# Moving the writes of turned tiles from SyncE's DMA queue to ScalarE's, and exchanging two PSUM banks

## Chip, core and metric

The kernel runs on one core of one Trainium2 chip. The metric is device time in microseconds (us) of one execution. Engines are named as in the profile: PE is TensorE (PEld its weight loads), DVE is VectorE, ACT is ScalarE, POOL is GpSimd and SP is SyncE. A "q" behind an engine's name (SPq) means its sequencer, which issues DMAs.

## What is computed

The input `x` is 128 graphs of 128 nodes with 512 features, in float32; `adj` is one 128x128 adjacency matrix for all of them. Two layers follow each other, each of the form "normalise, ReLU, graph operation, add to the input":

```python
# layer 0: graph convolution
h = relu(layernorm(x))
x = x + norm_adj @ (h @ W) + b          # norm_adj = D^-1/2 adj D^-1/2
# layer 1: attention with 8 heads of 64, masked by the adjacency
h = relu(layernorm(x))
q, k, v = h @ Wq + bq, h @ Wk + bk, h @ Wv + bv
a = softmax(q @ k.T / 8 + (1 - adj) * -1e9)
x = x + (a @ v) @ Wo + bo
```

## The kernel before

**Tiling.** A graph is one *element* of the batch. Four elements make a *group* (`GB = 4`), and there are 32 groups. The five 512x512 projections of a group are done by a Winograd form of Strassen's scheme (seven block products, most of them with seven products inside again), so that PE does fewer multiplications, and DVE and POOL do the additions.

**Order.** The schedule is written by hand. For each slot `t` the program runs five blocks, W, Q, K, V and Y: W is the graph convolution's product for group t+1, Q, K and V are the attention projections of group t, and Y is the output projection of group t-1. Each block has seven steps, 0 to 6, and each step has places for other work before it (`"Q3"`), between its two parts (`"Q3b"`) and after them (`"Q3c"`). The table `plan` says what else is done at a place: `at(t, "Q3c", f, ...)` appends a call. So five groups are in the air at a time: while PE projects group t, the softmax of group t-1 ends, its attention matrices are turned, and at V0 they are multiplied with v (`attend`, L943), right after K's last step and right before the scores of group t (`scores`, L868).

**Turning.** The attention product needs the attention matrices with keys on the partitions. Instead of transposes on PE, most groups are turned in two halves. `flip_att` (L917, L918) has DVE transpose all 32x32 blocks of the element's 128x1024 tile `att`, and then writes the tile to a DRAM buffer (`turned<-att`, one DMA of 512 KB). `turn_att` waits for that write and reads it back with the blocks exchanged (`att<-turned`, four DMAs of 128 KB by `from_dram`, L789, whose runs in DRAM are 32 floats long). The normalised input h of the attention layer is turned in the same way for two elements at a time: `flip_h` (L776, L778) and `turn_h`, with the DRAM buffers `h_dram` (`turned_h<-att`, `turned_h<-op_o`, `op_h<-turned_h`). Group 0 turns elements 2 and 3, and the last group all, on PE.

**DMA.** All DMAs are issued by SP, in program order: the turned writes and reads, five parts of 512 KB of each of the four weights for every group (`w<-wd_q` and so on, L1133), two loads of `x` (L177) and two stores of the result (L962). An instruction that waits on SP holds up all DMAs behind it. The built program also gives its DMAs eight completion semaphores in turn, and each DMA waits until the one eight places before it in the program has landed, whichever engine issued it.

**Banks.** There are eight PSUM banks: a0, a1, d0, d1, b, c with fixed names, and two small ones that take turns (`small_bank`). `attend` runs over the elements in the order 2, 0, 1, 3. Elements 2 and 3 write to a small bank, element 0 to bank b and element 1 to the a-bank that K's step 5 used last. Before PE may write bank b or that a-bank, DVE must have added K's results in them to `k`: these reads are L481 (parts of a bank) and L496 (a whole bank), at the end of block K. ACT copies the attention products out of PSUM (`fill`, L407). The scores of element 1 then go to bank b and the same a-bank, and those of element 3 to the two small banks.

**ACT in block Q.** In this order: two copies of q (L811), the statistics of an `x` tile (L340 and L341, twice), copies of q, two ReLUs with the normalisation (`gcn_norm`, L372, `h<-op_o`), two more pairs of statistics, copies of q and of `op_a` (L407), the third ReLU. `gcn_mix` on PE (tile `pa`, L142) reads each of those h.

Of the kernel before, what the change touches and what calls it, by code (L numbers as in the profile page):

```python
# [97 lines left out]
def kernel(  # L98
# [16 lines left out]
    nc = tc.nc  # L115
# [6 lines left out]
    NG = B // GB  # L122
# [21 lines left out]
    def small_bank(name):  # L144
        return ps_t.tile([P, 512], F32, tag="bank", name=name)
# [4 lines left out]
    bank = {k: ps_c.tile([P, 512], F32, tag=f"bank_{k}", name=f"bank_{k}") for k in ("a0", "a1", "d0", "d1", "b", "c")}  # L150
    turn = [0]
# [7 lines left out]
    att_dram = [dp.tile([P, H * P], F32, tag=f"turned_{b}", name=f"turned_{b}") for b in range(GB)]  # L159
    h_dram = [dp.tile([P, H * P], F32, tag=f"turned_h_{y}", name=f"turned_h_{y}") for y in range(2)]  # L160
# [609 lines left out]
    def flip_h(g, b):  # L770

        half, j = divmod(b, 2)
        h2 = hs.pop((g, b)).rearrange("n (c i f) -> n c i f", c=NC, i=4)
        t = op_att.t[:, SLOTS - 12 : SLOTS - 4, :] if half else att_of(g - 2, 2 if g > 2 else 1)
        t = t.rearrange("p s n -> p (s n)")
        nc.vector.transpose(t.rearrange("n (i c j f) -> n j c i f", i=4, c=NC, j=2)[:, j], h2)  # L776
        if j:
            nc.sync.dma_start(h_dram[half], t)  # L778

    def turn_h(g, half):  # L780
        op_h[g] = op_norm
        first = LEFT_AT[S1 if half else A11]
        from_dram(op_norm.t[:, first : first + 8, :], h_dram[half])
# [46 lines left out]

    maxima, sums = {}, {}

    def att_of(g, b):


        return att_buf[(b if g == 0 else b + 4 - 2 * g) % (GB + 1)]

    def by_blocks(g, b):  # L840

        return 0 < g < NG - 1 and not turned_in_place(g, b)

    def weights_of(g, b):

        return att_of(g, b - 1 if 0 < g < NG - 1 else b)

    def turned(g, b):

        if turned_in_place(g, b):  # L850
            return weights_of(g, b)
        return att_of(g, b - 2 if g else b - 1)

    def turned_in_place(g, b):

        return g == NG - 1 or g == 0 and b >= 2
# [55 lines left out]
    def flip_att(g, b):  # L912

        t = turned(g, b).rearrange("q h k -> q (h k)")
        order = "q h (i k) -> q h i k" if by_blocks(g, b) else "q h (k i) -> q h i k"
        dst = t.rearrange("q (i h k) -> q h i k", i=4, h=H)
        nc.vector.transpose(dst, weights_of(g, b).rearrange(order, i=4))  # L917
        nc.sync.dma_start(att_dram[b], t)  # L918

    def turn_att(g, b):  # L920
        from_dram(turned(g, b), att_dram[b])
# [10 lines left out]
    def attend(g, b):  # L932
        if g not in op_o:
            op_o[g] = op_norm if g == NG - 1 else op_att
        aT = turned(g, b)
        if b == 2 or b == 3:
            po = small_bank(f"po_{g}_{b}")
        else:
            po = bank["b" if b == 0 else f"a{1 - turn[0]}"]
        for c in range(NC):  # L940
            for p in range(2):
                h = 2 * c + p
                nc.tensor.matmul(  # L943
                    po[p * HD : (p + 1) * HD, c * P : (c + 1) * P],
                    vs[g][:, b, h * HD : (h + 1) * HD],
                    aT[:, p * NC + c, :],
                    start=True,
                    stop=True,
                )
        op_o[g].fill(nc.scalar.copy, b, po)  # L950
# [18 lines left out]
    def at(slot, place, f, *args):  # L969
        plan.setdefault((slot, place), []).append((f, *args))  # L970

    for t in range(-1, NG + 1):


        last = t == NG - 1
        if 0 <= t - 1 < NG - 1:
            g = t - 1

            for first, final, place, f, *args in (
                ("W4", "-Y6c", "W1c" if t == 2 else "-Y6c", flip_att, 0),  # L980
                ("W6", "Q2", "W4" if t == 2 else "W3", turn_att, 0),
                ("Q4c", "Q1c", "Q0b", flip_att, 1),
                ("Q6", "Q3", "Q2b", turn_att, 1),
                ("W6", "-Y3", "-Y3", exponentials, 2, 0, H // 2),
                ("Q3c", "-Y4", "-Y4", exponentials, 2, H // 2, H),
                ("Q6b", "-Y5b", "W0c" if t == 2 else "-Y5b", softmax_end, 2),
                ("K0c", "-Y5", "-Y5", exponentials, 3, 0, H // 2),
                ("K1c", "-Y6", "-Y6", exponentials, 3, H // 2, H),
                ("K3c", "W0", "W2", softmax_end, 3),
                ("K1", "Q2c", "Q2c", flip_att, 2),  # L990
                ("K3", "Q4", "K0", turn_att, 2),
                ("K3", "Q3c", "Q4b", flip_att, 3),
                ("K5", "Q5", "K0b", turn_att, 3),
            ):
                place = first if t == 1 else final if last else place
                if f in (flip_att, turn_att) and turned_in_place(g, args[0]):
                    continue
                at(t - place.startswith("-"), place.strip("-"), f, g, *args)
            if t == 1:
                at(1, "K4", transpose_att, g, 2)  # L1000
                at(1, "K6", transpose_att, g, 3)
            for b in (2, 0, 1, 3):
                at(t, "V0", attend, g, b)
        if t == 0:

            at(0, "Q0b", ln2, 1, 0)
            at(0, "Q1b", ln2, 1, 1)
            at(0, "K6", norm_h, 1, 0)
            at(0, "K6", norm_h, 1, 1)
            at(0, "V4", transpose_h, 1, 0)  # L1010
            at(0, "V4", norm_h, 1, 2)
            at(0, "V5", transpose_h, 1, 1)
            at(0, "V5", norm_h, 1, 3)
            at(1, "W0", transpose_h, 1, 2)
            at(1, "W1", transpose_h, 1, 3)
            at(1, "W1b", attention_operands, 1)
            at(2, "Q5", attention_residual, 1, 0)
            at(2, "K1", attention_residual, 1, 1)
        elif 1 <= t + 1 < NG and t >= 0:
            g = t + 1  # L1020
            at(t, "Q3b" if g < NG - 1 else "Q0b", ln2, g, 0)
            at(t, "K0b" if g < NG - 1 else "Q3b", ln2, g, 1)
            if g == NG - 1:

                places = ("Q3", "Q4", "Q5", "Q5", "Q6", "Q6", "K1", "K2", "K2")
                steps = ((norm_h, 0), (norm_h, 1), (transpose_h, 0), (norm_h, 2), (transpose_h, 1), (norm_h, 3))
                steps += ((transpose_h, 2), (transpose_h, 3))
            else:
                places = ("K1c", "K2c", "K4c", "K5b", "K3", "K4b", "K6b", "K6b", "Y6b")
                if t == 1:  # L1030
                    places = ("K2c", "K3c", "K6", "K6b", "K4b", "K5b", "V0b", "V0b", "Y6b")
                steps = ((norm_h, 0), (norm_h, 1), (norm_h, 2), (norm_h, 3))
                steps += tuple((flip_h, b) for b in range(GB))
                for half in range(2):
                    at(t, ("V3", "Y0")[half], turn_h, g, half)
            for place, (f, b) in zip(places, steps):
                at(t, place, f, g, b)
            at(t, places[8], attention_operands, g)
            at(t + 1, "Q3", attention_residual, g, 0)
            at(t + 1, "Q4", attention_residual, g, 1)  # L1040
# [3 lines left out]
        if 3 <= t + 2 < NG:  # L1044
            place = (t - 1, "Y6b") if t > 1 else (t, "W0")
            at(*place, load_x, t + 2, (0,), t > 1)
            at(*place, load_x, t + 2, (1,), t > 1)
        if 2 <= t + 2 < NG:
            g = t + 2
# [13 lines left out]
        if 0 <= t < NG:  # L1063
            g = t
# [30 lines left out]
        if last:  # L1095
            g = t
            at(t, "Y0", row_max, g, 2)

            at(t + 1, "W0", combine_w, "o last", nc.gpsimd)
            at(t, "Y1", exponentials, g, 2, 0, H)  # L1100
            at(t, "Y1b", row_max, g, 3)
            at(t, "Y2b", softmax_end, g, 2)
            at(t, "Y3", exponentials, g, 3, 0, H)
            at(t, "Y4b", softmax_end, g, 3)
            at(t, "Y6", transpose_att, g, 2)
            at(t + 1, "W0", transpose_att, g, 3)
            for b in range(GB):
                at(t + 1, "W0", attend, g, b)
            at(t + 1, "W0", output_operands, g)

            at(t + 1, "Y4", store_half, g, 0, slice(0, 256))
            at(t + 1, "Y5", store_half, g, 0, slice(256, 512))
            at(t + 1, "Y6", store_half, g, 1, slice(256, 512))
# [204 lines left out]
```

## Time and profile before

| | |
|---|---|
| median of 3 runs | 2262.12 us (2257.41 to 2262.69) |
| the profiled execution | 2243.55 us, of which the core's span is 2241.8 us; granted PE clock 0.999 |
| PE busy | 2200.8 us (98% of the span) |
| DVE, POOL, ACT busy | 1884.1 us (84%), 1868.6 us (83%), 1285.5 us (57%) |
| SP's DMA queue | 594.20 MB; its packets took 91.2% of 16 DMA engines' span |
| one group, from attention product to attention product | 67.9 to 68.2 us in 17 of the 27 of the steady stretch, 69.2 to 70.6 us in the other 10 |

The row of the profiled execution is what the profile's views describe; its time is below the three timed runs by 18.57 us at the median. "Idle before" in the views is time in which the engine did nothing before an instruction, and behind "<-" stands what ended most of it. Lines are of the kernel before.

### The profile page before, as it was taken

To read this page: it belongs to the slowest core of one execution; us is meant where nothing else is said; L and a number is where in the kernel's file an instruction comes from. 1 tells how busy PE (TensorE), PEld (TensorE's weight loads), DVE (VectorE), ACT (ScalarE), POOL (GpSimd) and SP (SyncE) were. 2 spreads that over 40 slices of the span, in tenths; PEclk is the share of its full clock that TensorE was granted. 3 is DMA by queue.
4 is the path that set the end of the run, shared out by engine and by line. 5 is a ranking of instruction groups with operands and counts; after the bars stand their busy time and mean duration, and the time that the engine had idled before them with its cause. 6 is when DMAs were issued, how large, how long until landed. Compare 5 with 4: busy or idle time off the path is not lost.

```text
span 2241.8 us, 78690 instructions
## 1 busy us (share of the span) xinstructions
PE 2200.8 (98%) x31597; PEld 1877.0 (84%) x31597; DVE 1884.1 (84%) x4252; ACT 1285.5 (57%) x3813; POOL 1868.6 (83%) x1994
## 2 busy tenths in 40 slices
PE   9989999999999999999999999999999999999999
PEld 6777888888888888888888888888888888888887
DVE  7787888888888888888888878888888888888886
ACT  3566655656556556566565575655665655756444
POOL 6898888888888988889888888888898888898764
PEclk9999999999999999999999999999999999999999
DMA  5389999999999999999999999999999999999994
GB/s 162 142 259 274 276 292 272 252 279 273 297 283 284 262 263 293 257 298 262 286 268 294 272 249 293 266 301 272 284 272 291 268 295 283 271 282 284 259 251 173
DMA packets 908108, 599.23 MB, mean 267 GB/s; under 512 B 765664, under 2 KB 772960, under 8 KB 907104
## 3 DMA queue, kind: packets, MB, share of 16 engines
q1 hardware_dynamic: 907744, 594.20, 91.2%
q8 instruction: 250, 4.10, 0.8%
q14 instruction: 114, 0.93, 0.1%
HBM read 455.68 MB, written 138.41 MB: 265 GB/s over the span
## 4 chain that ended last, share of the span: by engine, by line
PE 81%; DVE 7%; DMA 6%; SPq 3%; issue 1%; POOL 1%; ACT 1%; DVEq 0%; POOLq 0%
PE bank_a L142 31%; PE bank_d L142 18%; PE bank_b L142 10%; PE bank_c L142 9%; PE pa L142 4%; SPq L789 3%; DVE k L481 3%; PE bank_d L868 3%; DMA turned<-att 3%; DMA att<-turned 2%; PE po L943 2%; DVE q L481 2%; PE pss L868 1%; PE bank_b L868 1%; PE bank_b L943 1%
## 5 line engine op out<-in xcount | busy, mean ns | idle before, releaser
L899 ACT ACTIVATE att<-att,nmx 128x128 f32<-128x128 f32 x1024 | 402.9, 506 | 2.2 <-DVE nmx L887 1.5
L910 POOL TENSOR_TENSOR att<-att,rsm 128x1024 f32<-128x1024 f32 x121 | 229.5, 1897 | 149.3 <-DVE rsm L904 124.5
L142 PE MATMUL bank_a<-op_h,w 128*64 128x256 f32 x2976 | 352.8, 379 | 0.0
L811 ACT ACTIVATE q<-bank_a,bqk 128x256 f32<-128x256 f32 x192 | 79.9, 466 | 438.7 <-PE bank_a L142 438.7
L481 DVE TENSOR_TENSOR xt<-xt,bank_d 128x512 f32<-128x512 f32 x610 | 270.6, 468 | 11.8 <-PE bank_d L142 0.8
L142 PEld LDWEIGHTS bank_a<-op_h,w 128*64 128x64 f32 x2976 | 207.5, 137 | 81.6 <-issue 0.2
L94 POOL TENSOR_TENSOR op_o<-op_o 128x256 f32<-128x256 f32 x297 | 213.9, 739 | 27.2 <-DVE v L481 10.2
L142 PE MATMUL bank_d<-op_h,w 128*64 128x128 f32 (+1 forms) x3424 | 221.7, 275 | 0.0
L899 ACT ACTIVATION_READ_ACCUMULATOR att<-att,nmx 128x1 f32 x1024 | 211.0, 206 | 0.0
L94 POOL TENSOR_TENSOR op_a<-op_a 128x256 f32<-128x256 f32 x279 | 197.9, 733 | 15.1 <-ACT v L825 5.4
L142 PEld LDWEIGHTS bank_d<-op_h,w 128*64 128x64 f32 x3424 | 195.1, 137 | 6.7 <-issue 0.2
L94 POOL TENSOR_TENSOR op_h<-op_h 128x256 f32<-128x256 f32 x270 | 191.0, 731 | 9.4
L372 ACT ACTIVATE h<-xt,nb,rs 128x512 f32<-128x512 f32 x142 | 173.3, 1226 | 16.9 <-POOL nb L357 15.2
L142 PE MATMUL bank_a<-w,op_o 128*64 128x256 f32 x1536 | 182.2, 379 | 0.0
L142 PE MATMUL bank_a<-w,op_h 128*64 128x256 f32 x1488 | 178.0, 381 | 0.0
L142 PE MATMUL bank_a<-w,op_a 128*64 128x256 f32 x1488 | 176.5, 379 | 0.0
L496 DVE TENSOR_TENSOR xt<-bank_a,xt 128x512 f32<-128x512 f32 x252 | 165.9, 679 | 2.8 <-PE bank_a L142 2.8
L825 ACT COPY v<-bank_a 128x512 f32<-128x512 f32 x96 | 56.2, 585 | 181.9 <-PE bank_a L142 143.4
L887 DVE TENSOR_REDUCE nmx<-att 128x8 f32<-128x1024 f32 x128 | 152.5, 1209 | 0.6 <-POOL att L883 0.6
L917 DVE STREAM_TRANSPOSE att<-att 128x1024 f32<-128x1024 f32 x122 | 152.5, 1250 | 0.3 <-ACT att L899 0.2
L875 DVE SCALAR_TENSOR_TENSOR att<-bank_d,msk 128x512 f32<-128x512 f32 x128 | 82.4, 685 | 82.8 <-PE bank_d L868 82.7
L377 POOL TENSOR_TENSOR xt<-xt,b_o 128x1024 f32<-128x1024 f32 x62 | 147.5, 2381 | 0.0
(198 smaller groups left out, 5851.1 us busy)
## 6 DMA issues: line engine op xcount, KB each, us to landing
w<-wd_v SPq DMA_DIRECT2D x155, 512.0 KB, 6.5
w<-wd_o SPq DMA_DIRECT2D x155, 512.0 KB, 9.9
w<-wd_q SPq DMA_DIRECT2D x150, 512.0 KB, 5.3
w<-wd_k SPq DMA_DIRECT2D x150, 512.0 KB, 7.6
turned<-att SPq DMA_DIRECT2D x122, 512.0 KB, 5.2
att<-turned SPq DMA_DIRECT2D x488, 128.0 KB, 4.0
out_dram<-xt SPq DMA_DIRECT2D x62, 512.0 KB, 5.0
op_h<-turned_h SPq DMA_DIRECT2D x232, 128.0 KB, 4.9
```

Source lines behind the costliest of these rows:

```text
L94: engine.tensor_tensor(twice(out), twice(x), twice(y), ALU.subtract if minus else ALU.add)
L142: nc.tensor.matmul(out[y : y + P // 2], lhsT[:, y : y + P // 2], rhs, **flags)
L372: nc.scalar.activation(dst, src, AF.Relu, bias=nb[:, j : j + 1], scale=rs[:, j : j + 1])
L377: engine.tensor_tensor(t, src, bias.unsqueeze(1).to_broadcast([P, t.shape[1], D]), ALU.add)
L481: nc.vector.tensor_tensor(dst, dst, src, f)
L496: nc.vector.tensor_tensor(t, src.rearrange("p (r f) -> p r f", r=2), t, ALU.add)
L868: nc.tensor.matmul(pss[p][:, c, :], qs[g][rows, c, cols], ks[g][rows, c, cols], start=True, stop=True)
L875: nc.vector.scalar_tensor_tensor(dst, pss[p], SCALE, mask, ALU.mult, ALU.add)
L887: nc.vector.tensor_reduce(nmx, att_of(g, b), AX.X, ALU.max, negate=True)
L899: nc.scalar.activation(dst, src, AF.Exp, bias=nmx[:, h : h + 1], scale=1.0, accum_out=sm[:, h : h + 1])
L910: engine.tensor_tensor(att, att, rsm.unsqueeze(2).to_broadcast([P, H, P]), ALU.mult)
L917: nc.vector.transpose(dst, weights_of(g, b).rearrange(order, i=4))
```

## The change

All turned writes from the second group on, and the writes of turned h from the fourth group's h on, are taken from SP and issued by ACT. The DVE transposes stay where they are. A new function `write_turned` issues a write at a place of its own: for the attention of elements 0 to 3 at Y6c of the slot before, and at Q1, Q3c and Q5 (for the first such group W3 instead of Y6c; for the last one Y6c, Q2c, Q3c, Q4c), for h at K5b and V0. Before, SP had them at the places of the transposes, elements 0 to 3 at Y6c, Q0b, Q2c and Q4b. In the built program 176 DMAs go from SP's stream to ACT's; PE, DVE and POOL have the same instructions in the same order. The order of the elements in `attend` stays 2, 0, 1, 3, but element 0 now writes to a small bank and element 3 to bank b (in all groups but the last).

```diff
@@ flip_h
-        if j:
+        if j and g == 2:
             nc.sync.dma_start(h_dram[half], t)
+        elif j:
+            turned_to_dram["h", half] = t
+
+    def write_turned(kind, n):
+
+        dram = h_dram if kind == "h" else att_dram
+        nc.scalar.dma_start(dram[n], turned_to_dram.pop((kind, n)))
@@ flip_att
-        nc.sync.dma_start(att_dram[b], t)
+        if g == 0:
+            nc.sync.dma_start(att_dram[b], t)
+        else:
+            turned_to_dram["att", b] = t
@@ attend
-        if b == 2 or b == 3:
+        if b in ((2, 3) if g == NG - 1 else (0, 2)):
             po = small_bank(f"po_{g}_{b}")
         else:
-            po = bank["b" if b == 0 else f"a{1 - turn[0]}"]
+            po = bank[f"a{1 - turn[0]}" if b == 1 else "b"]
@@ the plan
                 at(t - place.startswith("-"), place.strip("-"), f, g, *args)
+                if f == flip_att and t > 1:
+                    b = args[0]
+                    place = (("-Y6c", "Q2c", "Q3c", "Q4c") if last else ("W3" if t == 2 else "-Y6c", "Q1", "Q3c", "Q5"))[b]
+                    at(t - place.startswith("-"), place.strip("-"), write_turned, "att", b)
@@ the plan, h of group t + 1
+            if 1 < t and g < NG - 1:
+                at(t, "K5b", write_turned, "h", 0)
+                at(t, "V0", write_turned, "h", 1)
```

More of the change, by code (lines that the diff above doesn't have):

```diff
@@ L827, in values @@
         return Projection(lambda: op_h[g], "v", region, False, first, g > 0).steps()
-    maxima, sums = {}, {}
+    maxima, sums, turned_to_dram = {}, {}, {}
     def att_of(g, b):
```

## The prediction

> **What bounds the kernel now.** I read the page first, then PE's groups with their shapes, SP's waits, the windows from one attention product to the next, and last the timeline around two of these products. The page's lines on engines, queue and chain:
>
> ```profile
> PE 2200.8 (98%) x31597; PEld 1877.0 (84%) x31597; DVE 1884.1 (84%) x4252; ACT 1285.5 (57%) x3813; POOL 1868.6 (83%) x1994
> ...
> q1 hardware_dynamic: 907744, 594.20, 91.2%
> ...
> PE 81%; DVE 7%; DMA 6%; SPq 3%; issue 1%; POOL 1%; ACT 1%; DVEq 0%; POOLq 0%
> ...
> turned<-att SPq DMA_DIRECT2D x122, 512.0 KB, 5.2
> ```
>
> PE is the bound: of 2241.8 us it is idle in 41.0. DMA is the next one, with 91.2%. Where PE is idle, by its groups (busy, mean ns | idle before):
>
> ```profile
> L943 PE MATMUL po<-att,v 128*64 128x128 f32 x1024 | 68.8, 277 | 21.2 <-DMA att<-turned 16.9 <-issue 3.8 <-PE bank_a L943 0.4
> ...
> L943 PE MATMUL bank_b<-att,v 128*64 128x128 f32 x512 | 35.4, 280 | 4.4 <-DVE k L481 4.4
> ```
>
> So 25.6 us of the 41.0 lie before the attention products, 21.2 of them before elements 2 and 3, whose matrices come late from DRAM. Why late, by SP's own waits (total, times, longest):
>
> ```profile
> SPq L789 <- DMA turned<-att: 286.4, 90, 9.0
> ```
>
> SP stands 286.4 us waiting for turned writes to land before it can read them back. The windows between attention products show what it costs (PE, PEld, DVE, ACT, POOL busy; clock; DMA share; GB/s):
>
> ```profile
> 902.77:972.47 69.70, 67.86 (x993) 58.41 (x993) 58.88 (x135) 40.22 (x119) 58.83 (x64) 1.00 0.95 272
> ...
> 1041.94:1109.86 67.92, 67.65 (x997) 58.38 (x995) 58.62 (x135) 40.24 (x119) 58.54 (x63) 1.00 0.95 279
> ...
> sum 1852.37, PE 1830.44 PEld 1578.02 DVE 1579.18 ACT 1085.75 POOL 1582.32; mean PE 67.79 PEld 58.45 DVE 58.49 ACT 40.21 POOL 58.60
> ```
>
> There are 27 such windows in the steady stretch. 17 take 67.9 to 68.2 us, 10 take 69.2 to 70.6. The late ones have the same work; DMA is not full in them (0.95), it waits. SP's timeline in a late one:
>
> ```profile
> 935.03 0.34 SPq L918 DMA_DIRECT2D turned<-att  x1
> ...
> 945.64 2.97 SPq L789 DMA_DIRECT2D att<-turned  x4
> ...
> 961.35 2.17 SPq L918 DMA_DIRECT2D turned<-att  x2
> ...
> 965.92 6.85 SPq L789 DMA_DIRECT2D att<-turned  x8
> ```
>
> Element 0's write takes 10.6 us to land, behind the loads of x and weights that SP issued before. All that follows on SP is late by that: the transposes of elements 2 and 3 end at 952.11 and 955.16 on DVE, yet their writes go out at 961.35, because the read of element 1 stands before them on SP. Their reads begin at 965.92, and the last one lands after PE wants it.
>
> **The change, part by part.** *The 176 moved writes.* On SP they go away: per group six issues of 0.319 to 2.250 us (median 0.377), and with them SP's wait for the transpose. No SP instruction is on PE's path except through landings. On ACT, the write of element 0 finds ACT idle (14.34 us before the next copy of q). It no longer queues behind SP's backlog. How long a write takes to land in a queue of its own no row shows. The bounds are 2.7 us (shortest landing of a turned tile in the trace) and the median 5.2 us. I take 4.2, the median over turned writes and reads together, which is nearest to a write with little before it. Then element 0's read can begin at about 939 instead of 945.64. The write of element 2 goes out at its place on ACT, when the two `h<-op_o` are under way (951.75 to 953.27): 8 us before 961.35. Element 3's goes out behind two more pairs of statistics, at about 956: 6 us earlier. Their reads still stand in SP's order and take 6.85 to 7.60 us of issue. Lateness at PE is 3.4 us at most in one group, so 4 to 6 us earlier covers every group: the 10 late windows become like the others, if DMA has the time. Its share of 0.93 to 1.01 of 67.9 us leaves 5 us to nothing. I therefore expect a few groups to stay late and keep 2.7 us of the stalls.
>
> [...] No run here has shown two queues.
>
> *What ACT pays.* Per group 6 x 0.377 = 2.3 us of issue, on an engine busy 40.2 of 67.9 us. The writes at Y6c, K5b and V0 lie where it idles (14.34 us, and 3.26 us before the first attention copy). Those at Q1, Q3c and Q5 (1.1 us) lie in a stretch that is full:
>
> ```profile
> 957.71 0.82 ACT L372 ACTIVATE h<-op_o,nb,rs 128x512 f32<-128x512 f32 x1 [0.17 <-POOL nb L354]
> ```
>
> This third h ends at 958.53, and PE's next `pa` starts at 958.73: 0.20 us of slack. The price lies between 0 (the sequencer issues while the activation before it runs) and 1.1 - 0.2 = 0.9 us per group, 25 us over 28 groups. ACT's rows start before the one before has ended (953.70 against 953.18 + 0.62), so its sequencer runs ahead. I take 0.1 us per group, 3 us. Queued behind each write on ACT are copies of q that DVE adds to, statistics that POOL's `nb` waits for, and that h.
>
> *The new waits on ACT.* Each write waits for its transpose (which ends before ACT arrives, by the times above) and for the DMA eight places before. For element 2 that is the second of three `w<-wd_k`. In the clean group it is issued at 1017.80 and lands 6.9 us later, at 1024.7, while ACT arrives by 1024.48. After the change it no longer stands behind element 1's write (issued at 1017.42, when its transpose ended) and goes out right after 1014.91, so it lands near 1022: no wait. I cost it at nothing; the cover is these 2 us, and every microsecond without it goes to PE.
>
> *The exchange of banks.* In a clean group PE waits at bank b, but DVE reads the a-bank right after it:
>
> ```profile
> 1042.80 0.41 DVE L481 TENSOR_TENSOR k<-k,bank_b 128x256 f32<-128x256 f32 x1
> ...
> 1043.26 0.85 PEld L943 LDWEIGHTS bank_b<-att,v 128*64 128x64 f32 x16 [0.51 <-DVE k L481]
> 1043.26 1.09 PE L943 MATMUL bank_b<-att,v 128*64 128x128 f32 x16 [0.27 <-DVE k L481]
> 1043.32 0.68 DVE L496 TENSOR_TENSOR k<-bank_a,k 128x512 f32<-128x512 f32 x1
> ...
> 1044.18 1.04 PE L943 MATMUL bank_a<-att,v 128*64 128x128 f32 x16
> ```
>
> With element 0 in a small bank, element 1 would reach the a-bank at 1043.69, but DVE leaves it at 1044.00. It starts at 1044.05 instead of 1044.18. So the 4.4 us at bank b mostly turn into a wait at the a-bank; 0.13 us per group is gained. Element 3 in bank b is read by ACT 0.78 us after its last matmul begins to drain, and the scores need that bank 0.9 us after: no wait, but little room.
>
> *Sum,* against the profiled execution. The 27 windows would take 27 x (67.91 - 0.13) = 1830.1 instead of 1852.37: 22.3. The stall before the first of them is 3.4. Less 2.7 for groups that stay late and 3 for ACT: 20.0 us, 2223.6 from 2243.55. The timed runs are 18.57 us above that execution. If this is a constant, the median becomes 2242.1. If it is ten more late groups at about 1.8 us each, it goes too: 2223.6. No view decides between them, and I take the middle, 2233.
>
> **The rivals.** *ACT is held (slower).* If weights land later in the timed runs than in the clean group, element 2's write holds ACT. In the late group that `w<-wd_k`, issued at 950.79, lands 7.4 us later at 958.2, and ACT arrives at 953.27: 4.9 us. Beyond 0.2 us it all falls on `pa`. At 1.5 us per group: 28 x 1.3 = 36 us lost against 20 gained, 2278. It decides from 20 / 28 + 0.2 = 0.9 us per group. For it: the slack of 0.2 us. Against it: the weights come earlier too, as their hold-up was element 0's read.
>
> [...]
>
> *DMA is full anyway (no change).* The bytes are the same. If the engines have no time left, as the share of 0.97 to 1.01 in several clean groups may mean, reads get later as writes get earlier, and only the banks' 28 x 0.13 = 3.6 us remain: 2258.5. Against it: the late windows have 0.93 to 0.96, less than the clean ones.
>
> **How the numbers follow.** About 0.3% (6.8 us) is what a measurement can tell from no change. Forecast 0.74, full DMA 0.10, held ACT 0.16. The low end is all stalls gone and the excess with them, 2243.55 - 25.7 = 2217.9; the high end takes in the second rival and a held ACT at break-even, 2262. That leaves out the held ACT beyond it.
>
> **What would show it.** Right: `turned<-att` under ACTq landing in under 5.2 us; SP's 286.4 us much smaller; `po<-att,v` idle 21.2 down to 5 or less; all windows near 67.8; bank b's idle gone and some 0.2 us before `bank_a<-att,v`. Wrong: `pa` or q's banks waiting for ACT, or windows still at 69 to 70 us with the reads as late as now.

## The result, and the profile after

The changed kernel takes 2294.62 us at the median (2292.56 to 2297.75), the kernel before 2259.76 us (2255.82 to 2262.69) on the same chip: 1.0157 times as long, with a 95% interval of 1.0134 to 1.0179. It is slower by 34.86 us, where 2233 us, a gain, were predicted. The profiled execution took 2295.67 us (span 2293.9 us, granted PE clock 0.994), 52.1 us more than the profiled one of before. The timed medians differ by less because the kernel before's profiled execution (2243.55 us) is some 16 us below the median that it has here; which part of the 52.1 us the timed executions lack is not shown.

The page's lines on engines, queues (q1 is SyncE's, q10 ScalarE's), chain and writes of turned tiles:

```profile
PE 2219.5 (97%) x31597; PEld 1885.8 (82%) x31597; DVE 1885.7 (82%) x4252; ACT 1292.5 (56%) x3813; POOL 1868.0 (81%) x1994
...
q1 hardware_dynamic: 882400, 501.91, 77.7%
q10 hardware_dynamic: 25344, 92.29, 10.3%
...
PE 69%; DVE 13%; DMA 7%; ACT 4%; issue 2%; POOL 2%; SPq 2%; ACTq 0%; DVEq 0%; POOLq 0%
...
turned<-att ACTq DMA_DIRECT2D x120, 512.0 KB, 6.0
```

At the median the writes land in 6.0 us from a queue of their own, where they took 5.2 behind everything on SyncE. PE is busy for 18.7 us more with the same matmuls, and idle for 33 us more. PE's groups, with their shapes (busy, mean ns | idle before):

```profile
L142 PE MATMUL bank_d<-op_h,w 128*64 128x128 f32 x3360 | 220.8, 278 | 0.0
L142 PE MATMUL pa<-ant,h 128*64 128x128 f32 x2032 | 134.7, 282 | 48.2 <-ACT h L372 48.2
L953 PE MATMUL po<-att,v 128*64 128x128 f32 x1024 | 61.5, 273 | 0.0
L953 PE MATMUL bank_a<-att,v 128*64 128x128 f32 x512 | 34.9, 278 | 5.3 <-DVE k L496 5.2
L953 PE MATMUL bank_b<-att,v 128*64 128x128 f32 x512 | 33.7, 274 | 6.3 <-DMA att<-turned 4.7 <-issue 0.9 <-DMA turned_h<-att 0.7
```

The 21.2 us before `po` are gone, and bank_a waits 0.19 to 0.20 us in 26 of 28 groups, as predicted. But `pa` waits 48.2 us for the third h, where it waited 2.8. SP waits longer than the 286.4 us of before, not less:

```profile
SPq L796 <- DMA turned<-att: 407.8, 61, 11.0
```

Three of the windows between attention products (PE, PEld, DVE, ACT and POOL busy; clock; DMA share; GB/s), and the sum over the same 27 as before:

```profile
428.81:500.60 71.79, 69.53 (x997) 59.95 (x994) 58.70 (x135) 40.82 (x119) 58.53 (x63) 0.98 0.92 276
...
850.93:923.55 72.62, 69.53 (x996) 59.96 (x994) 58.70 (x135) 40.61 (x119) 60.16 (x64) 0.98 0.93 274
...
1066.10:1134.72 68.62, 67.86 (x997) 58.29 (x995) 58.69 (x135) 39.70 (x119) 58.59 (x63) 1.00 0.94 275
...
sum 1904.53, PE 1848.34 PEld 1586.51 DVE 1584.13 ACT 1093.53 POOL 1582.59; mean PE 68.46 PEld 58.76 DVE 58.67 ACT 40.50 POOL 58.61
```

The sum is 52.2 us above before (1904.53 - 1852.37), which is all of the difference between the two profiles. PE's busy time has 17.9 us of it (1848.34 - 1830.44). The rest is idle time: 45.4 more before `pa`, 5.3 before bank_a, 1.9 more before bank_b, 21.2 less before `po`, and small waits.

Why h is late is seen in ScalarE's timeline of the second of these windows (start, duration; in brackets the idle time before):

```profile
899.78 1.52 ACT L372 ACTIVATE h<-op_o,nb,rs 128x512 f32<-128x512 f32 x2 [0.23 <-POOL nb L354]
903.98 0.34 ACTq L785 DMA_DIRECT2D turned<-att  x1
904.42 0.63 ACT L340 ACTIVATE unused<-op_o 128x512 uint8<-128x512 f32 x1 [3.11 <-DVE q L481]
...
908.96 0.81 ACT L372 ACTIVATE h<-op_o,nb,rs 128x512 f32<-128x512 f32 x1 [0.17 <-POOL nb L354]
```

Two h are done at 901.30. Then ScalarE stands until 903.98, when it issues element 2's write. In the built program this write waits for the second of three `w<-wd_k`, which SP issued at 894.99; the trace has it landing at 903.90. The element's transpose, the write's other condition, had ended on DVE at 900.13. The releaser printed with the 3.11 us (DVE) is only the one that the profile saw last; nothing DVE does then is new. The group shown is no exception: in all 27 groups of the steady stretch element 2's write is issued 0.08 us after its own `w<-wd_k` has landed, and in 22 of them ScalarE stands idle until then, for 37.0 us in all. The statistics, and with them the third h, are late by that. On PE in the same window:

```profile
909.82 1.64 PE L142 MATMUL pa<-ant,h 128*64 128x128 f32 x16 [2.90 <-ACT h L372]
911.25 1.93 PE L142 MATMUL bank_d<-op_h,w 128*64 128x128 f32 x16
```

After the 2.90 us of waiting, the next sixteen matmuls of bank_d take 1.93 us, where such a set takes 1.04 elsewhere. That is where most of PE's extra busy time comes from: in 8 of the 27 windows the granted clock is 0.98 and PE is busy for some 69.5 us instead of 67.86.

### The profile page after: what moved, and what is told of

It is laid out like the page before. It is cut to its first block, busy times and chain, and to the rows that moved or that the text cites. A ratio compares the mean times of both kernels' runs of the same rounds, so it can differ in the third digit from the quotient of the medians.

```text
span 2293.9 us, 78538 instructions
## 1 busy us (share of the span) xinstructions
PE 2219.5 (97%) x31597; PEld 1885.8 (82%) x31597; DVE 1885.7 (82%) x4252; ACT 1292.5 (56%) x3813; POOL 1868.0 (81%) x1994
## 3 DMA queue, kind: packets, MB, share of 16 engines
q1 hardware_dynamic: 882400, 501.91, 77.7%
q10 hardware_dynamic: 25344, 92.29, 10.3%
## 4 chain that ended last, share of the span: by engine, by line
PE 69%; DVE 13%; DMA 7%; ACT 4%; issue 2%; POOL 2%; SPq 2%; ACTq 0%; DVEq 0%; POOLq 0%
PE bank_a L142 25%; PE bank_d L142 17%; PE bank_b L142 9%; PE bank_c L142 8%; DVE q L481 4%; PE pa L142 3%; DVE k L481 3%; PE bank_d L875 3%; DVE att L924 2%; DMA att<-turned 2%; SPq L796 1%; DVE st L343 1%; PE bank_b L953 1%; DMA w<-wd_v 1%; PE bank_a L953 1%
## 5 line engine op out<-in xcount | busy, mean ns | idle before, releaser
L818 ACT ACTIVATE q<-bank_a,bqk 128x256 f32<-128x256 f32 x192 | 79.9, 466 | 446.7 <-PE bank_a L142 438.1
L142 PE MATMUL bank_d<-op_h,w 128*64 128x128 f32 (+1 forms) x3424 | 228.4, 280 | 0.0
L142 PEld LDWEIGHTS bank_d<-op_h,w 128*64 128x64 f32 x3424 | 201.8, 141 | 6.8 <-DVE q L481 0.2
L142 PE MATMUL pa<-ant,h 128*64 128x128 f32 x2032 | 134.7, 282 | 48.2 <-ACT h L372 48.2
L142 PEld LDWEIGHTS pa<-ant,h 128*64 128x64 f32 x2032 | 117.9, 141 | 67.1 <-ACT h L372 62.2
## 6 DMA issues: line engine op xcount, KB each, us to landing
w<-wd_o SPq DMA_DIRECT2D x155, 512.0 KB, 10.2
```

The lines of the kernel that those rows point to most:

```text
L142: nc.tensor.matmul(out[y : y + P // 2], lhsT[:, y : y + P // 2], rhs, **flags)
L818: nc.scalar.activation(dst[:, r], src[:, r], AF.Identity, bias=bqk[:, i, oc : oc + 1], scale=1.0)
```

## Experiments

"Partner" below is the DMA eight places earlier in the built program, whose landing a DMA waits for before it is issued.

**The banks alone,** on the kernel before.

```diff
-        if b == 2 or b == 3:
+        if b in ((2, 3) if g == NG - 1 else (0, 2)):
             po = small_bank(f"po_{g}_{b}")
         else:
-            po = bank["b" if b == 0 else f"a{1 - turn[0]}"]
+            po = bank[f"a{1 - turn[0]}" if b == 1 else "b"]
```

> The exchange of banks alone, all writes on SyncE as before. My theory (ScalarE is held by the write of element 2, which waits for a weight's landing; the banks are innocent): 0 to 5 us below the kernel before, so some 2256 us; bank b's 4.4 us of idle time goes, about 5 us (28 times 0.19) appear before bank_a, the 21.2 us before po stay within 5 us. Rival (the exchange itself costs, since element 3's product and the scores now share bank b): 10 us or more above the kernel before, with idle time before bank_b's scores.

0.9986 (0.9968 to 1.0005): no measurable difference, and compatible with the 3.6 us that were predicted. Idle time before `po` and bank_b's products is 13.5 and 11.9 us; the sum is that of before (21.2 and 4.4), since the late last element now writes to bank_b. The banks are innocent.

**Element 2's write back on SyncE, in its new place.**

```diff
-        nc.scalar.dma_start(dram[n], turned_to_dram.pop((kind, n)))
+        queue = nc.sync if kind == "att" and n == 2 else nc.scalar
+        queue.dma_start(dram[n], turned_to_dram.pop((kind, n)))
```

> The changed kernel with element 2's write issued by SyncE, at the same place in the program; the five others stay on ScalarE. Theory of the hold: the 48.2 us before pa fall to 5 or less, PE's busy time returns from 2219.5 to about 2201, and the time is 40 to 55 us below the changed kernel, 2240 to 2255; some of the 21.2 us before po return (5 to 12), since this write again stands behind element 1's read on SyncE. Rival of the issues (six issues of 0.33 us on ScalarE cost the time): a sixth of the loss goes, 2285 to 2290. Rival of the transfers (two queues delay each other's landings): within 0.3% of the changed kernel.

1.0225 (1.0188 to 1.0261): slower still, against all three theories. PE's idle time before `pa` did fall, to 12.8 us, but other waits came:

```profile
ACT h L372 <- DMA att<-turned: 36.0, 13, 5.4
ACT q L819 <- DMA w<-wd_k: 9.3, 9, 2.3
```

These are ScalarE's waits. Element 3's write now has the third `w<-wd_k` as its partner, and the write of turned h stands for its own partner, the first read of element 3, which comes late (36.0 us); POOL then waits 79.9 us for `turned_h<-op_o`, and PE 14.4 us for POOL's `op_o`. The hold did not leave ScalarE, it changed its place. PE's busy time stayed at 2221.7 us where 2201 were expected, at a granted clock of 0.998; why is not shown. Taking one write away moves the partners of the writes after it; this run is no clean test of the issue.

**Element 2's write on ScalarE, but behind the third h,** right before element 3's.

```diff
-                    place = (("-Y6c", "Q2c", "Q3c", "Q4c") if last else ("W3" if t == 2 else "-Y6c", "Q1", "Q3c", "Q5"))[b]
+                    place = (("-Y6c", "Q2c", "Q3c", "Q4c") if last else ("W3" if t == 2 else "-Y6c", "Q1", "Q5c", "Q5c"))[b]
```

> The changed kernel with element 2's write still on ScalarE, but behind the third h, right before element 3's write. Theory of the hold: the weight part has landed by then and the third h stands before the write, so the idle time before pa falls to 5 us or less and the clock comes back; 40 us or more below the changed kernel, 2240 to 2255. Element 2's read begins some 5 us later than in the changed kernel, so 3 to 10 us of waiting before po may return. Rival of the issues: there are as many issues as before the edit, so within 0.5% of the changed kernel. Rival of the transfers: the same.

1.0102 (1.0074 to 1.0131). Idle time before `pa` falls to 3.1 us, as expected. The time falls by only 0.5% against the changed kernel, since the late reads are back:

```profile
L953 PE MATMUL po<-att,v 128*64 128x128 f32 x1024 | 62.1, 274 | 8.3 <-DMA att<-turned 6.7 <-PE bank_c L142 1.1
...
L953 PE MATMUL bank_b<-att,v 128*64 128x128 f32 x512 | 35.7, 281 | 30.8 <-DMA att<-turned 26.3 <-issue 4.5
```

39.1 us, against 25.6 before. With element 2's write behind the third h the two last writes go out only 0.7 and 1.0 us earlier than with the banks alone (means over 25 groups, counted from the group's attention product), and still the last read lands 1.2 us later. So moving the writes does not make the reads earlier by itself; something in it makes them later.

**A hold with no DMA:** three activations that nothing needs, on ScalarE at Q3c, all writes on SyncE.

```diff
+    def hold(n):
+        for _ in range(n):
+            nc.scalar.activation(unused, bo_bc, AF.Identity, bias=0.0, scale=1.0)
...
+                if f == flip_att and args[0] == 2 and 2 < t < NG - 1:
+                    at(t, "Q3c", hold, 3)
```

> The kernel before with all writes on SyncE, and three activations of 0.62 us that nothing needs on ScalarE in each of 28 groups, at the place where the changed kernel has element 2's write: a hold of 1.9 us with no DMA in it. Theory of the hold: 28 times (1.9 - 0.2) = 47 us of idle time before pa, most of the 21.2 us before po hidden by it, so about 26 us above the kernel before, plus up to 19 us if PE's clock falls after these stalls as it did in the changed kernel: 2286 to 2305. Rival of the transfers: a hold of this size does not reach PE, within 0.5% of the kernel before. If PE's busy time stays at 2201 with this much idle time before pa, the slower matmuls of the changed kernel do not come from the stall.

1.0132 (1.0107 to 1.0158), 2277.93 us where the kernel before takes 2249.24. PE's group and a typical window:

```profile
L142 PE MATMUL pa<-ant,h 128*64 128x128 f32 x2032 | 129.1, 274 | 46.9 <-ACT h L372 46.8
```

```profile
493.09:562.89 69.80, 67.86 (x996) 58.20 (x994) 58.75 (x135) 42.13 (x122) 58.60 (x63) 1.00 0.97 278
```

The 46.9 us were foreseen as 47: of a hold of 1.9 us at this place 1.66 go to PE, in 27 groups, and 2 us of the sum are older waits. A hold of 1.7 us per group costs what the changed kernel's idle time costs, with no write moved. All windows from 283.59 to 2098.50 us are within 0.1 us of 69.80, and waiting for att<-turned is down to 3.3 us: given 1.9 us more per group, the reads on SyncE are in time. So part of the 21.2 us that the changed kernel "saved" before `po` can be this, and no merit of the queue. PE is busy for 2204.7 us: these stalls of 1.66 us, about as many as in the changed kernel, hardly slow the matmuls (67.86 us of PE work in a window, 67.65 in a clean window of the kernel before).

**Element 1's write back on SyncE at Q0b.** This changes the partner of element 2's write to the fourth read of element 0.

```diff
-        if g == 0:
+        if g == 0 or b not in (0, 2, 3):
             nc.sync.dma_start(att_dram[b], t)
...
-                if f == flip_att and t > 1:
+                if f == flip_att and t > 1 and args[0] in (0, 2, 3):
```

> The changed kernel with element 1's write back on SyncE at its old place (Q0b), all else as changed. With this, the DMA eight places before element 2's write is no longer a part of w_k but the fourth read of element 0, which lands some 24 us before the attention product, long before ScalarE arrives; element 2's write stays on ScalarE at Q3c. Theory of the hold by the DMA eight places before: idle time before pa falls from 48.2 to 10 us or less (what is left comes from element 3's write, which now waits for the third w_k), and element 1's write, again ahead of the last two loads of w_k, lands in 6 us instead of 8.5. Time 0 to 20 us below the kernel before. Rival (the place on ScalarE and the issue are what costs): idle before pa stays at 35 to 50 us, and the time within 0.5% of the changed kernel, 1.2% above the kernel before.

1.0058 (1.0030 to 1.0086), 1% below the changed kernel; a gain on the kernel before, which was hoped for, is not there. Idle time before `pa` is 20.9 us, where 10 were allowed and the rival had 35 to 50. What is left sits at element 3's write, whose partner is now the third `w<-wd_k`. Element 2's write on ScalarE at Q3c no longer holds anything.

**One write or two at a time on ScalarE,** the banks exchanged in all. The edit is the one above with `(2, 3)`, `()`, `(1,)` and `(0,)`; where h is not moved, also

```diff
-        if j and g == 2:
+        if j:
             nc.sync.dma_start(h_dram[half], t)
...
-            if 1 < t and g < NG - 1:
+            if False:
                 at(t, "K5b", write_turned, "h", 0)
                 at(t, "V0", write_turned, "h", 1)
```

> The banks exchanged, and of the writes only those of elements 2 and 3 on ScalarE at Q3c and Q5; elements 0 and 1 and both of h on SyncE as before. If the hold comes from the DMA eight places before, and the late reads from element 1's write being overtaken by weight loads, neither is here: idle before pa under 10 us, writes of elements 2 and 3 go out 4 to 6 us earlier than before, waiting for att<-turned falls from 20 to under 8 us, and the time is 10 to 25 us below the kernel before. Rival (two queues slow each other's transfers, whichever write is moved): the landings grow, and the time is at or above that of the kernel before.

> The banks exchanged, and of the writes only the two of h on ScalarE; all four of attention on SyncE as before. Theory (the loss comes from elements 1 and 2): within 0.4% of the kernel before, no idle time before pa beyond 5 us; POOL's waiting for turned_h<-op_o rises from 7.8 to some 25 us off PE's path. Rival of the transfers (a write in a second queue lands later and holds its readers): 10 us or more above the kernel before.

> The banks exchanged, and of the writes only element 1's on ScalarE at Q1; the rest on SyncE as before. If the late reads of the changed kernel come from this write, which on SyncE stood ahead of the last two loads of w_k and on ScalarE shares the DMA engines with them: it lands in 8 to 9 us instead of 5.9, the reads of elements 1 to 3 come 2 to 4 us later, idle time before the products of elements 0 and 3 rises from 25 to 40 to 60 us, and the time is 15 to 35 us above the kernel before, with no idle time before pa beyond 5 us. Rival (all of the loss is the hold of ScalarE by element 2's write): within 0.4% of the kernel before.

> The banks exchanged, and of the writes only element 0's on ScalarE, at Y6c where ScalarE idles. My prediction had this land in 4.2 us and the read of element 0 begin 6 us earlier. By the changed kernel (it landed in 6.9 us there, on SyncE in 6.4 in the kernel before) it gains nothing: read of element 0 begins where it did, 29 to 30 us before the product, and the time is within 0.4% of the kernel before. If it costs (elements 0, 2, 3 and h moved took 0.6% more than before, 2 and 3 alone 0.7% less): 5 to 20 us above, with the read of element 0 or the parts of w_k later. No hold of ScalarE before pa in either case, 4 us or less.

| on ScalarE | against before | idle before pa | idle before po and bank_b's products |
|---|---|---|---|
| none, banks only | 0.9986 (0.9968 to 1.0005) | 1.7 us | 25.4 us |
| element 0 | 1.0057 (1.0039 to 1.0076) | 1.5 us | 27.7 us |
| element 1 | 1.0033 (1.0014 to 1.0051) | 1.3 us | 26.8 us |
| elements 2 and 3 | 0.9928 (0.9908 to 0.9948) | 14.1 us | 0.0 us |
| both of h | 0.9964 (0.9948 to 0.9980) | 2.1 us | 7.2 us |
| elements 0, 2, 3 and h | 1.0058 (1.0030 to 1.0086) | 20.9 us | 0.5 us |
| all six | 1.0157 (1.0134 to 1.0179) | 48.2 us | 6.3 us |

The change is two changes of opposite sign, and a hold that comes only with their combination. The single rows do not add up to 1.6%: element 2's write has a `w<-wd_k` as partner only where element 1's write has left its place in the count; in those with element 2 on ScalarE and element 1 on SyncE the partner is a read of element 0, which has landed at least 1 us before. Elements 2 and 3 are what the prediction wanted: in that kernel the writes go out 18.9 and 15.2 us before the group's attention product, where they left at 12.6 and 11.9 with the banks alone (means over 25 steady groups), and no product waits for a read. 25 of the 27 windows of the steady stretch are like the first one here, 67.84 us; the second is one of the other two, which have a hold each (`pa` waits 14.1 us in the whole kernel, where under 10 were expected):

```profile
355.29:423.13 67.84, 67.64 (x997) 58.37 (x994) 58.65 (x135) 40.21 (x119) 58.56 (x63) 1.00 1.00 282
423.13:499.23 76.10, 70.50 (x997) 60.86 (x995) 58.74 (x135) 40.61 (x119) 61.45 (x66) 0.96 0.93 264
```

Its ScalarE timeline shows the hold alone, with the releaser named:

```profile
482.08 0.33 ACTq L785 DMA_DIRECT2D turned<-att  x1
482.46 0.84 ACT L818 ACTIVATE q<-bank_a,bqk 128x256 f32<-128x256 f32 x2 [5.89 <-DMA w<-wd_k]
```

The third `w<-wd_k`, element 3's partner, landed at 482.01, and element 3's write was issued at 482.08. ScalarE was idle for 5.89 us, with copies of q and the third h behind it. The 67.84 us windows have both writes in ScalarE's tight stretch, so the issue itself costs PE nothing. The writes of h alone were expected to be neutral; the waits before the products fall to 7.2 us with them, which no run explains, and the time cannot be told from that of the banks alone (the intervals overlap).

No run put the writes of elements 2 and 3 ahead of element 1's read within SyncE's own order. Whether the gain needs a second queue, or only the earlier place, is open.

Elements 0 and 1 lose, element 1 less than expected (7 us where 15 to 35 were, with 26.8 us of waits where 40 to 60 were). Alone, element 0's write lands after 7.5 us instead of 6.6 with the banks alone, and element 1's after 7.4 instead of 6.1, each issued within 0.3 us of its time on SyncE; the reads behind them start 0.8 and 1.6 us later (means over the same groups). In one group of the kernel with element 1 moved, the write is issued at 740.90 between a `w<-wd_k` (740.72) and a `w<-wd_v` (741.32), and the three land at 749.76, 749.50 and 750.85. In the kernel with 2 and 3 moved, where SyncE issues element 1's write ahead of the last two `w<-wd_k`, it lands in 4.9 us (746.07 to 750.97) and they follow at 752.16 and 753.64. So here the write in a second queue was under way together with weights that would have stood behind it, and took 8.9 us. That this explains the whole 0.5 to 0.7% is not shown: the profiles have 1 to 2 us more idle time before the products, and the spans are 5 and 7 us longer.

**Element 3's write later,** on the kernel with 2 and 3, and then with h on ScalarE too.

```diff
-                    place = (("-Y6c", "Q2c", "Q3c", "Q4c") if last else ("W3" if t == 2 else "-Y6c", "Q1", "Q3c", "Q5"))[b]
+                    place = (("-Y6c", "Q2c", "Q3c", "Q4c") if last else ("W3" if t == 2 else "-Y6c", "Q1", "Q3c", "Q5c"))[b]
```

> As the kernel with the writes of elements 2 and 3 alone on ScalarE, but element 3's write behind the third h (Q5c). There it waits for the first part of w_v instead of the third of w_k, and the third h stands ahead of it. Theory of the hold: the three groups with 3.2 to 5.4 us before pa become like the others (67.84 us), idle before pa 4 us or less, PE's busy time 2201 or less; 1% to 1.6% below the kernel before, 2215 to 2225 us where that takes 2246. Rival (the later write brings back late reads): waiting for att<-turned rises to 10 us or more and the time is not below 2229.

> The same with both writes of h on ScalarE too, so that only the writes of elements 0 and 1 are left on SyncE. If the moved writes of h are neutral: within 0.3% of the kernel with elements 2 and 3 alone, 1% or more below the kernel before. If each further write on the second queue slows the others: 0.4% or more above it, with a longer wait of POOL for turned_h<-op_o (12.4 us where h alone was moved, 39.0 us with element 0 too).

0.9965 (0.9951 to 0.9979) and 0.9931 (0.9909 to 0.9953). The first is a miss: 17.9 us remain before `pa`. Behind the third h the write has the first part of `w<-wd_v` as partner, which comes late in 13 of the 27 groups and there holds the fourth h instead (ScalarE stands 2.4 us behind the write on the mean). With h moved as well, 4.4 us remain; the time is that of the kernel with 2 and 3 alone, as expected, but not 1% below the kernel before. That kernel and the one with 2 and 3 at their first places are the best measured, 0.7% below the kernel before, and no interval tells them apart.

**A longer hold,** in the kernel with all writes on SyncE.

```diff
-                    at(t, "Q3c", hold, 3)
+                    at(t, "Q3c", hold, 5)
```

> The kernel before with five instead of three activations that nothing needs, so that ScalarE is held some 3.2 us in each of 28 groups. If the slower matmuls of the changed kernel come from the length of PE's stall: idle before pa of about 28 times 3 = 84 us, and PE's busy time rises by 1.5 us or so in many of the 28 groups (20 to 45 us in all), where it did not rise with stalls of 1.66 us: 2330 to 2355. If length is not what counts, PE's busy time stays near 2204 and the time is about 2310 to 2318.

1.0553 (1.0519 to 1.0586), 2370.63 us, above the range. Idle time before `pa` is 82.9 us as expected, and PE's busy time is 2261.5 us, 56.8 more than with three. Two windows that follow each other:

```profile
432.10:506.10 74.00, 70.75 (x996) 61.12 (x994) 58.73 (x135) 43.73 (x124) 61.37 (x66) 0.95 0.94 267
506.10:578.89 72.79, 69.54 (x997) 59.95 (x995) 58.75 (x135) 43.73 (x124) 57.37 (x61) 0.98 0.89 255
```

All 27 groups have the same stall of 2.98 us. Most alternate between 70.7 and 69.5 us of PE work at clocks of 0.95 and 0.98, where 1.66 us of stall left 67.86 at 1.00. Length counts.

**Only the partners changed:** all writes on ScalarE as in the changed kernel, and small DMAs that shift the count of eight.

```diff
+    def tiny():
+        for d in tiny_dram:                 # three, or six, tiles of 1x128
+            nc.sync.dma_start(d, ident[0:1, :])
...
+                if f == flip_att and args[0] == 1 and 2 < t < NG - 1:
+                    at(t, "Q0c", tiny)
```

> The changed kernel with three DMAs of 512 bytes that nothing needs, issued by SyncE in each of 28 groups at Q0c, ahead of the last two parts of w_k. They move the count of the semaphores, but not so that it matters: element 2's write on ScalarE still waits for the second of the three w_k, element 3's for element 1's write. Control for the next kernel: idle before pa stays at 45 us or more, the time within 0.6% of the changed kernel, 1.2% to 2.2% above the kernel before. Rival (what counts is not the partner in the count): no difference between the two kernels.

> The same with six such DMAs instead of three: element 2's write now waits for the last of these small ones, which is issued and lands ahead of the last two parts of w_k; element 3's write waits for the third w_k. No write is moved to another queue or place. If the hold comes from the partner in the count of eight: ScalarE is no longer idle behind element 2's write; what is left is a shorter hold at element 3's write, as in the kernels with element 1's write on SyncE (14 to 21 us before pa), so idle before pa falls to 30 us or less, PE's busy time to 2212 or less, and the time is 0.7% or more below the kernel with three, though it has three more DMAs. Rival (the issues, or the sharing of the DMA engines): idle before pa stays at 45 us or more, the time at or above that with three.

Three of them: 1.0119 (1.0084 to 1.0154), 36.8 us before `pa`, less than the 45 expected, in a profiled execution that is the fastest of four (2266.39 us; the median is 2275.34). Element 2's write still waits for the second `w<-wd_k`, and goes out right after its landing in all 27 groups. Six: 1.0345 (1.0318 to 1.0373), where a gain was expected. The reason stands in PE's groups and ScalarE's timeline of the kernel with six:

```profile
L142 PE MATMUL bank_d<-op_h,w 128*64 128x128 f32 x3360 | 226.8, 283 | 62.8 <-DVE q L482 62.8
L142 PE MATMUL pa<-ant,h 128*64 128x128 f32 x2032 | 129.6, 275 | 10.2 <-ACT h L373 10.1
```

```profile
907.33 0.33 ACTq L786 DMA_DIRECT2D turned<-att  x1
907.70 0.84 ACT L819 ACTIVATE q<-bank_d,bqk 128x256 f32<-128x256 f32 x2 [4.47 <-DMA w<-wd_k]
```

Element 2's hold is gone: 10.2 us are left before `pa`. But the shift also gave element 1's write a part of w_k as partner, instead of a read of element 0. Now ScalarE stands at that write (4.47 us here), the copies of q behind it are late, DVE's additions after them, and PE waits 62.8 us before bank_d. The group is typical: in 26 of 27 groups ScalarE stands idle until element 1's write goes out, right after its partner's landing (75.8 us in all), and in none behind element 2's. With every write in the same queue and at the same place, PE's stall moved from one product to another with the partners. That settles the mechanism; the expected time was wrong because the partner of element 1's write was not looked at.

## Why the prediction was wrong

*What failed* is the sentence on the new waits on ACT: the wait for "the DMA eight places before" was costed "at nothing". The second `w<-wd_k` was to go out right after 1014.91, 9 us or more before ACT arrives at 1024.48, and to land 7 us later, with 2 us to spare. It does land 7.8 us after its issue (mean of the 27 groups; 8.9 in the group shown). But ACT reaches element 2's write 6.5 us after that issue, not 9. The load stands behind element 0's read on SP, here in the group shown above:

```profile
890.17 3.55 SPq L796 DMA_DIRECT2D att<-turned  x4
...
894.47 1.96 SPq L1150 DMA_DIRECT2D w<-wd_k  x3
```

In all 27 groups this read begins within 0.1 us of the landing of element 0's write. That write, issued by ACT at 883.07 here, was to land in 4.2 us; it takes 7.0 at the median and never under 6.2. In the clean group from which the prediction took its times it had landed in 4.8 us, where the median of the kernel before is 6.4. So the 2 us of cover came from one favourable group, and the weights did not "come earlier too". No longer behind element 1's write, the load leaves 4.7 us after element 0's write has landed instead of 5.9 (means), but that write takes longer to land. The idle time before `pa` that follows is 48.2 us, 1.7 per group on the mean.

The rival of a held ACT, with 1.5 us per group, its place and its partner, was the right case with a chance of 0.16; its break-even of 0.9 us per group was passed by far. That its 2278 us are within 17 us of 2294.62 is partly luck: in the profiles `pa` waits 45.4 us more (36 in the rival), the products 14 us less (20), and PE works 17.9 us longer, which the rival did not have.

*Not foreseen:* matmuls that run slower after the stall, 17.9 us in the 27 windows. The prediction costed a stall at its length alone. The stalls of 1.66 us did cost little more than their length (0.2 us of PE work); those of 2.98 us cost 1.7 to 2.9 us more than that.

*The size of the moved writes' gain.* "I take 4.2" for the landing rests on the author's estimate that a write in ACT's queue has little before it, which no run shows: 6.0 was measured, above the upper bound of 5.2, which came from the same write on SyncE. The bounds had no row for two queues at once, and a write in ACT's queue did not gain on the backlog in SP's: element 0's, issued right behind its transpose as before, took longer to land (7.0 against 6.4 us at the median). Against the kernel before, the writes of elements 2 and 3 left 5.5 and 3.3 us earlier (means over 25 groups; predicted 8 and 6), but the last read landed only 1.6 us earlier.

*Which moved writes gained.* Those of elements 0 and 1 gained nothing (0.6% and 0.3% are lost). Those of 2 and 3 did: the kernel with these two moved is 0.7% faster, and in it they no longer stand behind a wait for another element's write.

*The issues on ACT* take 326 ns at the median and at most 359; 93 of the 176 overlap an issue of SP, and they too are within 359. So an issue of SP at the same time lengthened them by 33 ns at most. Nor do they hold PE: 0.1 us per group was counted, and windows of 67.84 us with both writes in the tight stretch show nothing.

*What was right.* The stalls before the products came from late reads, and writing elements 2 and 3 from another queue takes them away: 25.4 us with the banks alone, 0.0 with these two. The banks: 0.19 us before bank_a, as derived. Full DMA was rightly held unlikely: the windows of 67.84 us run without a stall at shares of 0.92 to 1.00.

*The timed excess.* "No view decides" was true, and neither reading holds: the kernel before has 2246 to 2262 us as its medians on the chips used, and single executions from 2235.92 to 2262.69, so 18.57 us lie within the spread between executions and between chips.

## What to carry over

Here the writes given to ScalarE brought all of their waits to its stream, also that for a reused completion semaphore (37.0 us of ScalarE idle before element 2's writes). Before you move a DMA to a compute engine, look up in the built program which DMA it waits for, and when that one lands in the new order. Take such times from many groups, not from one that ran well. Here the writes that stood behind another wait in their queue gained, and those whose only neighbours were transfers lost (0.7% against 0.3 and 0.6%). Test such a change one write at a time, and list the partners again after every edit.

## What the runs showed of the hardware

- PE's clock after a short stall. Equal stalls of 1.66 us in 27 groups left a window's mean at 1.00 in all but the first (0.98). Stalls of 2.98 us lowered it to 0.95 or 0.98, in most groups alternately, with 2.9 or 1.7 us more PE work. In the changed kernel a stall of 2.04 us was followed by sixteen matmuls of bank_d in 1.92 us, at a granted clock of 0.57 in the 4 us from the stall's end, and one of 2.81 us by sixteen in 1.04 us, at 1.00. So the length of a single stall did not decide it in this kernel; what did is not shown.
- No more bandwidth was seen with two queues: with all six writes in ScalarE's queue the two shares are 77.7% and 10.3%, together below the 91.2% of one queue, in a longer span.
